# A graph network of four layers on one core: about half of the edges are sorted by source during the hops, and their messages take the source row by a one-hot product instead of a gather

## The chip, the cores and the metric

The kernel runs on one core of a Trainium2 chip. The metric is the time of one execution on the device in microseconds (us); the figure for the kernel before is the median of three executions. A core has five engines that run side by side and wait for each other by semaphores: TensorE (PE, matmuls; the loading of its weights is listed as PEld), VectorE (DVE), ScalarE (ACT), GpSimd (POOL) and SyncE (SP). Every engine takes its instructions in order. Transfers are issued from the queues of SP, ACT and POOL. The chip also grants PE a share of its full clock, which the profile records.

## The reference

Input: x of 3125 nodes by 96 features, 100000 edges (src, dst) sorted by dst, and 4 attributes per edge. Four blocks follow each other, each x = x + block(relu(layernorm(x))):

```
L0: out = h; ten times:  out = 0.9 * segment_sum(out[dst] * w, src) + 0.1 * h        ("hops")
L1: m = relu(h[src]) + eps;  a = softmax of m over the edges of each dst;  (h + segment_sum(a * m, dst)) @ W + b
L2: node    = batchnorm(relu(h @ W_node + b))
    edge    = batchnorm(relu(edge_attr @ W_edge + b))
    message = batchnorm(relu([h[src], h[dst], edge] @ W_msg + b))
    segment_sum(message, dst) + node
L3: two graph convolutions with a leaky relu between
```

L2 is where the change lies. The product with W_msg splits in three: P = h @ W_msg[:96] for the source, Q = h @ W_msg[96:192] + bias for the destination, and the edge's features times W3 (the last 96 rows with the batchnorm folded in). So each edge needs P[src] + Q[dst] + relu(edge_attr @ W_edge + b) @ W3. The sums over all edges that the batchnorm of the messages needs come from a Gram matrix.

## The kernel before

All of it is one function, `narrow`; a second one, `wide`, follows only where a flag says that the data break an assumption of the first (here it does not run). `narrow` has these stages:

- **Setup** (0 to some 440 us): edges are laid out as 98 rows ("quads") of 1024 edges. One-hots of source and destination are multiplied to count matrices (C8, and its transpose A8, in fp8). Tables for later are written to DRAM, among them ea_d (18 rows per edge: attributes as an fp16 high and low half and a one), rl_d and rlT_d (the destination's row within a quad) and srcT_d (the source).
- **Hops** (to 1088 us): L0 as ten products of A8 with the node features. `gather` (L379 to L391) runs 13 slots of two blocks of 128 nodes per step, each block 25 matmuls (L387). `onward` scales the result, and `beside` (L512) puts other work in the slots: the statistics of the edge features (L515 to L522), loading x, and a ReLU over A8 that checks for an overflow (L531). The lists of this and of the next stage are ordered by a scheduler. POOL has no work in this stage.
- **L1** (1088 to 1249 us): one loop over 25 blocks (L619). Each block also computes its rows of P and Q and writes them to the DRAM tables Pt and Qt (L661), as fp16 in two halves: high in columns 0 to 95, low in 96 to 191.
- **Messages** (1249 to 2477 us, L674 to L839), in an order written out by hand (L811 to L837). The 100000 edges are taken in 196 half quads of 512, four chunks of 128 edges each. For half quad i the calls are: `gather_rows(i)` issues four indirect transfers on POOL (L747), each fetching 128 rows of 384 bytes of Pt, five half quads ahead and into six buffers (pgs); `edge_features(i)` makes the features of 512 edges on PE, and ACT and DVE split them into an fp16 high and low half (eh L766, el L768); `messages(i)` runs six matmuls per chunk into PSUM (L781): three for the features times W3 (eh with W3's high and low half, el with the high half), one for Q by a one-hot of the destination (ohT) and two with an identity, which add the gathered halves of P. DVE takes the relu (m, L783), ACT and DVE split m again (L376, L377). `summed(i)` runs two half quads later: per chunk one matmul sums the messages by destination (segs, L801) and one adds to the Gram matrix (gram, L803). `load_quad(g)`, on SP's queue, loads what a quad needs: four pieces of Q (L734), the edge rows (L739) and the destination rows spread over 128 partitions (L741). After each quad the sums are written to the table Sd (L808); rows shared with the next quad are carried over by a small matmul (L800).
- **L3** (2477 us to the end): Sd is loaded, the batchnorm is applied, and two convolutions with C8 follow.

## Time and profile before

| | us |
|---|---|
| median of three runs | 2426.81 (2423.4 to 2430.7) |
| the profiled execution, its own time | 2647.15 |
| its span, first to last instruction | 2645.2 |
| PE busy / DVE / ACT / POOL | 2003.1 / 1433.2 / 870.8 / 808.4 |
| hops, 560 to 1140: PE busy | 573.4 of 580 |
| messages, 1350 to 2480: PE busy, POOL busy | 777.3 and 699.1 of 1130 |
| gathers on POOL (L747) | 784, mean 0.978, first 1248.8, last 2451.7 |

The profiled execution is a run of its own, and longer than the median. A row of the profile names the line, the engine, the operation, out<-in by the program's names, the shapes and the count; after the bar come busy time, mean ns of one, and the engine's idle time just before these instructions with what ended it ("issue": nothing that the profile shows). PE's matmuls overlap, so its busy time adds up overlapping durations only once, and the distance between starts says more than a duration. "Granted clock" is the share of PE's full clock.

### The profile page before, as it was taken

The page shows a single profiled execution, that of the slowest core. Times are in us where ns is not written, and L with a number is a line of the kernel's source. Part 1 is how long each engine was busy: PE and PEld are TensorE (multiplying, and loading weights), DVE is VectorE, ACT ScalarE, POOL GpSimd, SP SyncE. Part 2 cuts the span into 40 slices and gives each one's busy share as a digit, 9 for nine tenths or more (in the row PEclk, how much of TensorE's full clock was granted, in tenths as well). Part 3 has the DMA queues.
Part 4 walks back from the last instruction along what each step waited for, and adds up shares of the span by engine and source line. Part 5 has one row for each costly group of instructions (what it writes and reads, how often), then busy time and mean ns, then how long its engine had stood idle before and what let it go on. Part 6 is the DMA issues. An engine that isn't in the chain of part 4 may idle for free.

```text
span 2645.2 us, 47376 instructions
## 1 busy us (share of the span) xinstructions
PE 2003.1 (76%) x17758; PEld 1553.0 (59%) x17758; DVE 1433.2 (54%) x3971; ACT 870.8 (33%) x2136; POOL 808.4 (31%) x808
## 2 busy tenths in 40 slices
PE   0477777899999999997475666767776776667699
PEld 0222335788888899986354445555555555555488
DVE  2768999875655554876244333434333334334653
ACT  0398846479433311432121111112111111111340
POOL 4100000000000000000666566666666666666000
PEclk9889999999999999998566675556555556555599
DMA  2100000000000000101222222222222222222100
GB/s 74 56 14 1 1 1 1 6 9 10 9 10 10 10 20 2 25 18 26 61 65 68 49 64 68 65 69 64 65 68 65 68 65 68 65 68 65 31 1 21
DMA packets 118578, 100.90 MB, mean 38 GB/s; under 512 B 83532, under 2 KB 90454, under 8 KB 118338
## 3 DMA queue, kind: packets, MB, share of 16 engines
q1 hardware_dynamic: 91002, 54.80, 7.9%
q0 software_dynamic: 25088, 38.59, 6.4%
q10 hardware_dynamic: 2248, 4.40, 0.6%
q8 instruction: 141, 2.31, 0.4%
q14 instruction: 99, 0.81, 0.1%
HBM read 83.46 MB, written 14.21 MB: 37 GB/s over the span
## 4 chain that ended last, share of the span: by engine, by line
PE 39%; issue 18%; DVE 14%; ACT 8%; another core or an unknown queue 5%; SPq 0%; DMA 0%; ACTq 0%; DVEq 0%
PE hop L387 19%; PE pre L781 7%; PE segs L801 3%; DVE u L377 3%; ACT x L531 3%; ACT u L376 2%; PE gram L803 2%; DVE el L768 2%; PE ef L764 2%; DVE m L783 1%; PE eps L520 1%; ACT A L444 1%; PE hop L623 1%; DVE oh L757 1%
## 5 line engine op out<-in xcount | busy, mean ns | idle before, releaser
L747 POOL DMA_INDIRECT u<-Pt,srow x784 | 766.9, 978 | 590.3 <-issue 186.4
L387 PE MATMUL hop<-u,A 128*128 128x192 f16 (+1 forms) x6250 | 550.0, 247 | 3.1 <-DVE degs L481 1.4
L387 PEld LDWEIGHTS <-A 128*128 128x128 fp8e4 x6250 | 522.4, 98 | 48.3 <-issue 44.6
L783 DVE SCALAR_TENSOR_TENSOR m<-pre,cb 128x384 f32<-128x384 f32 x196 | 109.1, 557 | 577.6 <-PE pre L781 287.1
L376 ACT ACTIVATE u<-m 128x384 f16<-128x384 f32 x196 | 102.5, 523 | 881.9 <-issue 721.9
L801 PE MATMUL segs<-u,oh 128*128 128x194 f16 x784 | 239.6, 337 | 126.3 <-issue 76.1
L781 PE MATMUL pre<-u,ident 128*128 128x96 f16 x1568 | 275.8, 267 | 68.9 <-issue 68.0
L781 PE MATMUL pre<-W3h,eh 96*128 96x96 f16 x1568 | 279.8, 269 | 58.4 <-issue 56.9
L272 PE MATMUL cps<-hk,hl 128*128 128x500 f16 x784 | 232.5, 417 | 53.4 <-DVE hl L230 36.7
L803 PE MATMUL gram<-u 128*97 128x194 f16 x784 | 245.4, 344 | 5.4 <-issue 5.4
L230 DVE TENSOR_TENSOR hk<-ki,keyT 128x4000 f16<-128x4000 f16 x98 | 220.3, 2248 | 43.7 <-PE cps L272 27.2
L781 PE MATMUL pre<-qg,ohT 128*128 128x96 f16 x784 | 210.2, 268 | 33.0 <-issue 32.9
L781 PE MATMUL pre<-W3h,el 96*128 96x96 f16 x784 | 210.1, 268 | 30.4 <-issue 27.2
L781 PEld LDWEIGHTS <-eh 96*128 96x128 f16 x1568 | 178.4, 136 | 77.1 <-issue 74.5
L803 PEld LDWEIGHTS <-u 128*97 128x97 f16 x784 | 143.2, 183 | 123.2 <-issue 118.9
L589 POOL IOTA li<- 128x512 f16 x1 | 1.2, 1185 | 680.2 <-ACT exs L507 680.2
L781 PEld LDWEIGHTS <-ident 128*128 128x128 f16 x1568 | 164.9, 135 | 74.0 <-issue 73.9
L276 ACT ACTIVATE C<-cps 128x500 f32 x269 | 162.8, 605 | 91.6 <-PE cps L275 65.8
L801 PEld LDWEIGHTS <-oh 128*128 128x128 f16 x784 | 103.2, 132 | 126.6 <-issue 126.6
L377 DVE TENSOR_TENSOR u<-m,u 128x384 f16<-128x384 f32 x196 | 109.5, 559 | 115.6 <-ACT u L376 59.0
L272 PEld LDWEIGHTS <-hl 128*128 128x128 f16 x784 | 73.8, 119 | 166.1 <-DVE hl L230 77.5
L521 ACT ACTIVATE eps<-eps 96x512 f32<-96x512 f32 x196 | 106.2, 569 | 153.8 <-PE eps L520 145.3
(309 smaller groups left out, 3095.1 us busy)
## 6 DMA issues: line engine op xcount, KB each, us to landing
h<-rl_d SPq DMA_DIRECT2D x98, 256.0 KB
u<-Pt,srow POOLq DMA_INDIRECT x784
qg<-Qt SPq DMA_DIRECT2D x392, 12.0 KB
Sd<-sacc SPq DMA_DIRECT2D x98, 48.0 KB
x<-ea_d SPq DMA_DIRECT2D x195, 18.0 KB
et<-ea_d SPq DMA_DIRECT2D x97, 36.0 KB
et<-in_edge_attr_T ACTq DMA_DIRECT2D x4, 390.6 KB
ea_d<-eh SPq DMA_DIRECT2D x8, 195.3 KB
```

The costliest lines, as they stand in the source:

```text
L230: V.tensor_tensor(t, pat[:, None, :, :].to_broadcast([P, s, n, c]), val[:, q, :].rearrange("p (s c) -> p s c", s=s)[:, :, None, :].to_broa ...
L272: T.matmul(ps, hl[:, j // 4, :, j % 4], hk[:, j // 2, :, j % 2], start=j == js[0], stop=n == 0 and j == js[-1])
L276: S.activation(C8[:, :, bass.ds(column_of(g), WIN)], ps, AF.Copy)
L376: S.activation(hi, t, AF.Copy)
L377: V.tensor_sub(lo, t, hi)
L387: T.matmul(ps[:, i, :], table[:, k, c0 + (b0 + i) * P:c0 + (b0 + i + 1) * P], u[:, k, :], start=k == 0, stop=k == NB - 1)
L521: S.activation(ps, ps, AF.Relu)
L747: G.indirect_dma_start(out=pgs[i % len(pgs)][:, c, :], out_offset=None, in_=Pt, in_offset=bass.IndirectOffsetOnAxis(ap=srow[:, k:k + 1], a ...
L781: T.matmul(ps[:, c, :], t, w, start=j == 0, stop=j == 5)
L783: V.scalar_tensor_tensor(m, ps, 0.0, over_b(cb, HC), ALU.max, ALU.subtract)
L801: T.matmul(seg, oh[:, half, :, c], mm[:, c, :], start=half == 0 and c == 0, stop=last)
L803: T.matmul(gram, mm[:, c, :D + 1], mm[:, c, :], start=i == 0 and c == 0, stop=g == Q - 1 and last)
```

## The change

The first QA = 47 quads (48128 edges) are treated in a new way; the other 51 quads keep their gathers. The 47 quads form three groups GA of 125, 125 and 126 columns of 128 edges.

- **Sorting, during the hops.** `in_bins(g)` is a generator; from slot 13 on `beside` advances it by two steps per slot. Per group it loads src and dst, finds for each edge its bin (25 bins of 125 source rows) and its place in the bin by prefix sums along the rows (13 scans per group, two bins packed in a number) and over the partitions (a matmul with a triangle, tri16), and then POOL issues one indirect scatter per column: 128 records of 12 fp16 numbers (attributes, one, source row in the bin, destination row) to the DRAM table recs[g], 376 scatters in all. The records are blank elsewhere, so bins have spare places: a group fills 152 chunks instead of 125 or 126. Other residents of the scratch room in x shrink (the edge statistics are aggregated in four parts), and x is loaded in slot 106 instead of 91, on SP's queue instead of ACT's.
- **Turning, during L1.** `in_fields(g)` loads recs[g], transposes the records on PE in groups of four units and writes them to the table fields, up to three steps per block from blocks 2, 7 and 16 on. P is also loaded to SBUF in tiles of 125 rows (psb).
- **Messages.** There are now 216 units of four chunks in an alternating list: 114 of sorted edges ("A") and 102 of gathered half quads ("B"). In an A unit a chunk holds edges of a single bin, so P comes from two matmuls of a one-hot of the source (ohS) with psb. Its destinations fall in a window of 128 or 256 rows per slice of 25 chunks (18 slices; WIDE, 13 of one and 5 of two windows), so Q takes two matmuls per window and the sums one per window. Slices hand rows over to the next slice by a shifted product. For both kinds the edge features stay fp32 and take one fp32 matmul with W3 instead of three fp16 ones; eh and el are gone.
- **Around it.** Sums go to two tables Sd, added on POOL before L3. The flag is computed at the end of L1 instead of its start, and counts the edges placed. The mean of the messages is corrected for the EMPTY blank places.

```diff
+QA = 47
+GA = [(0, 125), (16000, 125), (32000, 126)]
+BINS, BN = 25, 125
+SL, CAP = 6, 768
+CG = 152
+UA = len(GA) * CG // 4
+WIDE = [1] * 13 + [2] * 5
...
+    def in_bins(g, rp, ep):
...
+        for i in range(13):
+            V.scalar_tensor_tensor(mv, t, float(i), w, ALU.is_equal, ALU.mult, accum_out=tot[:, i:i + 1])
+            if i % 4 == 3:
+                yield
...
+        T.matmul(ps, tri16, tots.rearrange("p a b -> p (a b)"), start=True, stop=True)
...
+        for i in range(13):
+            V.scalar_tensor_tensor(mv, t, float(i), w, ALU.is_equal, ALU.mult)
+            V.tensor_tensor_scan(scan, mv, mv, tot[:, i:i + 1], ALU.add, ALU.max)
+            V.copy_predicated(pos, mv.bitcast(I32), scan)
+            yield
...
+        for c0 in range(0, C, 14):
...
+            G.dma_start(et, ea[:, c0:c0 + n])
+            G.tensor_copy(r[:, :n, 0:4], et)
+            G.tensor_tensor(r[:, :n, 4:8], et, r[:, :n, 0:4], ALU.subtract)
+            G.tensor_copy(r[:, :n, 9:11], lane2[:, c0:c0 + n, :])
+            for c in range(n):
+                ins = G.indirect_dma_start(
+                    out=recs[g], out_offset=bass.IndirectOffsetOnAxis(ap=addr[:, c0 + c:c0 + c + 1], axis=0),
+                    in_=r[:, c, :], in_offset=None, bounds_check=P * CG - 1, oob_is_err=False)
...
-                        load_x()
...
+                    if slot == 106:
+                        load_x(nc.sync)
+                    for b in range(2 * (slot - 112), min(2 * (slot - 111), NB)) if 112 <= slot < 125 else ():
+                        V.scalar_tensor_tensor(x[:, b, :], hs[:, b, :], back[:, b:b + 1], x[:, b, :], ALU.mult, ALU.add)
+                    if slot >= 13:
+                        next(binning, None)
+                        next(binning, None)
...
-                    if 0 <= i < 50:
-                        S.activation(junk, A8[:, i // 2, i % 2 * (NP // 2):(i % 2 + 1) * (NP // 2)], AF.Relu, bias=late_top,
+                    for i in (2 * i, 2 * i + 1) if 0 <= i < 50 else ():
+                        S.activation(junk, A8[:, i // 4, i % 4 * (NP // 4):(i % 4 + 1) * (NP // 4)], AF.Relu, bias=late_top,
...
+        def in_fields(g):
+            r = lp.tile([P, CG, 12], F16, name="recs2", bufs=2)
+            nc.sync.dma_start(r.rearrange("p c k -> p (c k)"), recs[g].rearrange("(p c) k -> p (c k)", p=P))
...
+                for i in range(n):
+                    T.matmul(ps[:, i, :], rf[:, u0 + i].rearrange("p f j -> p (f j)"), ident16,
+                             start=True, stop=True)
+                t = wp.tile([44, 4, P], F16, name="fts")[:, :n, :]
+                S.activation(t, ps, AF.Copy)
...
+            for j, (first, per) in enumerate(((2, 3), (7, 3), (16, 3))):
+                for _ in range(per if b >= first else 0):
+                    next(turning[j], None)
...
+        UB = (Q - QA) * 2
+        units = sorted([((i + 0.4) / UA, 0, i) for i in range(UA)] + [((i + 0.6) / UB, 1, i) for i in range(UB)])
...
+            for r in (0, 9):
+                nc.sync.dma_start(et[r:r + 9, :], fields[i, :36].rearrange("(f j) e -> f (j e)", f=9))
+            sp = wp.tile([P, 2, HC * P], F16, name="spread", bufs=5)
...
-            eh = wp.tile([D, HC * P], F16, name="eh")
-            S.activation(eh, ps, AF.Relu)
-            el = wp.tile([D, HC * P], F16, name="el")
-            V.scalar_tensor_tensor(el, ps, 0.0, eh, ALU.max, ALU.subtract)
+            feat[n] = wp.tile([D, HC * P], F32, name="efs")
+            S.activation(feat[n], ps, AF.Relu)
...
+                by = [(feat[n][:, cs], W3)]
+                if kind:
+                    pg = pgs[i % len(pgs)]
+                    by += [(hot[n][0][:, cs], quad[QA + i // 2][1][:, i % 2, :]), (ident16, pg[:, c, :D]), (ident16, pg[:, c, D:])]
+                else:
+                    k, s, _, _ = chunk(i, c)
+                    by += [(hot[n][2][:BN, cs], psb[:, k, hl * D:(hl + 1) * D]) for hl in range(2)]
+                    by += [(hot[n][0][:, v, cs], slices[s][1][:, v, hl * D:(hl + 1) * D]) for v in range(WIDE[s]) for hl in range(2)]
...
+            for n in range(L + 2):
+                if n + 1 < L:
+                    edge_features(n + 1)
+                    one_hots(n + 1)
+                if n >= 2:
+                    summed(n - 2)
+                if n < L:
+                    messages(n)
+                if n % 6 == 5:
+                    node_piece(n // 6)
+                if n + 5 < L:
+                    fetch(n + 5)
+                if n < L and units[n][0] and units[n][1] + 5 < UB:
+                    gather_rows(units[n][1] + 5)
...
+            for t, d in ((sd, Sd[0]), (sd2, Sd[1])):
+                nc.sync.dma_start(t[:, b:b + 5, :], d[b * P:(b + 5) * P].rearrange("(b p) d -> p b d", p=P))
+            G.tensor_tensor(sd[:, b:b + 5, :], sd[:, b:b + 5, :], sd2[:, b:b + 5, :], ALU.add)
```

## The prediction

> **What bounds the kernel now.** I read the page first (spans and the forty slices), then the stages by window, then the gather's row, then POOL and PE in order of time inside the message stage.
>
> ```profile
> span 2645.2 us, 47376 instructions
> POOL 4100000000000000000666566666666666666000
> PEclk9889999999999999998566675556555556555599
> L747 POOL DMA_INDIRECT u<-Pt,srow x784 | 766.9, 978 | 590.3 <-issue 186.4
> L387 PE MATMUL hop<-u,A 128*128 128x192 f16 (+1 forms) x6250 | 550.0, 247 | 3.1 <-DVE degs L481 1.4
> ...
> 330.00:480.00 150.00, 113.64 (x942) 69.63 (x941) 141.99 (x322) 89.42 (x243) 0.12 (x1) 0.97 0.00 1
> 560.00:1140.00 580.00, 573.40 (x6275) 519.78 (x6273) 354.06 (x1254) 249.00 (x577) 1.19 (x1) 1.00 0.05 12
> 1140.00:1250.00 110.00, 92.84 (x967) 81.50 (x964) 76.78 (x404) 33.08 (x102) 1.15 (x1) 0.94 0.07 18
> 1350.00:2480.00 1130.00, 777.26 (x6303) 579.15 (x6303) 440.12 (x884) 209.12 (x467) 699.12 (x715) 0.59 0.26 64
> ...
> L747 POOL DMA_INDIRECT u<-Pt,srow x784: 938/944/1372, 1248.8 to 2451.7; - x196
>   DMA Qt<-hv: 153.4, 1
> ...
> 1264.44 0.94 POOL L747 DMA_INDIRECT u<-Pt,srow  x1 [0.30 <-issue]
> 1265.69 0.94 POOL L747 DMA_INDIRECT u<-Pt,srow  x1 [0.30 <-issue]
> ```
>
> The slices show two halves. Up to 1250 us PE works at full clock and POOL does nothing; afterwards POOL issues 784 gathers and PE runs at a granted clock of 0.59. The windows give, in their columns, the length and the busy time of PE, PEld, DVE, ACT and POOL, then the granted clock. In the hops (560 to 1140) PE is the limit, 573 of 580 us. In the message stage no engine is full by this account, so the cadence has to be read: a gather holds POOL 0.944 us and the next starts 0.30 us later, 1.245 us apart whenever nothing is waited for. 784 of them need 976 us; they took 1204 (1248.8 to 2451.7, and the last one).
>
> The difference is of a peculiar kind:
>
> ```profile
> 1263.58 0.24 PE L781 MATMUL pre<-qg,ohT 128*128 128x96 f16 x1 [1.17 <-issue]
> 1265.00 0.24 PE L781 MATMUL pre<-u,ident 128*128 128x96 f16 x1 [1.19 <-issue]
> 1267.10 0.24 PE L781 MATMUL pre<-u,ident 128*128 128x96 f16 x1 [1.85 <-issue]
> ...
> 2520.73 0.80 PE L883 MATMUL op<-W_g,zT 96*128 96x96 f32 x4
> 2521.36 0.25 PE L387 MATMUL hop<-u,C 128*128 128x192 f16 x1
> ```
>
> Here PE, waiting for nothing that is named, steps through single matmuls 1.4 to 2 us apart, and POOL then waits for PE to hand back a gather buffer. POOL's idle time is 590.3 us; without the 153.4 before its first gather and 784 x 0.30 between them, 202 us of such waiting remain. The profiled execution took 2647.15 us, 220 above the median of 2426.81. I take the two for the same thing, an effect of tracing in the stage with the most transfers: 2647 - 202 = 2445, and with 0.944 for the mean of 0.978 per gather 2418; the median lies between them. So without tracing the message stage is taken to last about 1000 us (976 of gathers and 23 from the last gather to the last gram matmul), bound by POOL's cadence. Measured time is predicted as the median of 2427 less what changes.
>
> **The change part by part.**
>
> Removed: the gathers of 47 quads. 784 become 51 x 8 = 408, 408 x 1.245 = 508 us over 216 units (114 of sorted edges, 102 gathered half quads). POOL stops being the limit; PE is next. Two fp16 weight halves and the DVE step L768 (678 ns) go, and one fp32 matmul per chunk takes the place of three fp16 ones.
>
> PE per unit, at full clock. The hops give 550.0 us for 6250 matmuls of 192 columns, 88 ns, so 44 for 96 columns and about 250 for 512. For the fp32 matmul the rows above have the same shape: four records, two products, from 2520.73 to 2521.36, 0.31 us each.
> - Gathered: 0.25 + 4 x (0.31 + 3 x 0.044) + 8 x 0.088 + 0.15 for the carry = 2.87 us.
> - Sorted, window of one: 0.25 + 4 x (0.31 + 4 x 0.044) + 0.70 = 2.89.
> - Sorted, window of two (the last five slices, 32 units): 0.25 + 4 x (0.31 + 6 x 0.044) + 12 x 0.088 = 3.61.
> - 102 x 2.87 + 82 x 2.89 + 32 x 3.61 = 646; 17 slice hand-overs of some 0.9 and the node pieces bring 671. PE was busy 84% of the L1 window, 99% of the hops; I take 92%: 730, and 15 to start and drain: **745 us in place of 1000, -255**.
>
> [...] The trace shows two loads per product and 0.31 us; I take that[...].
>
> Other engines beside PE: DVE, from m 557, lo 559 (L377), oh 683/2 plus overhead 0.42, ohT about 0.33 per 512 columns: 1.99, 2.2 and 2.8 us for the three kinds, 473 us, with the 0.59 us wait for ACT between m and lo 600. ACT 1.1 a unit, 240. SP issues some 2 us of transfers per sorted unit and 4.9 per quad (3.19 for the four qg, 0.33, 1.04, 0.35): 478 us. All lie below 671, five units ahead or two behind. DVE is the nearest.
>
> Hops: 376 scatters of 128 rows, and 27 small loads with three POOL steps. POOL was idle there. Nearest row: the gather, 1.245; with 1.85 for each load and its steps (POOL's cast and subtract of 1000 elements took 1.2 and 2.1 us, these have 56) 468 + 50 = 518 us, 575 if each load's landing (2.1 us) is waited for. In program order they begin near 605 (slot 24, 4.56 us a slot) and end at 1125 to 1180. Two things wait for them: the load of x, SP, at slot 106 (979 us; group 1 must be read, 605 + 250 x 1.245 + 35 = 951) and the third in_fields, b = 16 (1182 us; SP's load and then ACT's copy wait, and PE behind them). Both fit, the second by 2 to 57 us. The bounds for a scatter: none below the gather's 1.245[...]. In the trace, [...]the mean gather is 34 ns over its median, 13 us in all. I take the trace's value and nothing exposed; the range has 0 to 100.
> DVE adds some 265 steps of 126 elements, 0.22 us each (neighbouring fp32 steps 0.15 to 0.31): 58 us, in stretches where it idles 40%. If that cover fails, hop matmuls wait for its PSUM reads. Four offset matmuls wait for DVE with PE's hops queued behind them, 1 to 3 us each: **+8**. Halving the ReLU scan (L531) adds 50 fixed costs to ACT, which is full only from 555 to 675: in the 8. The later x load and x update have 27 us between them, for 1.2 MB (5 us at q1's 262 GB/s): nothing, or 5.
> L1: 29 groups of four transposes on PE (6 us) and an ACT copy each, with one PSUM buffer, so 0.8 us may be exposed each time; PE also loses a hop buffer: 5 to 30, **+15**. The flag and its DVE passes (3 us) now precede the messages: **+4**. The second Sd load and POOL's five adds stand before x += sd: **+5**. Bigger zero fills and blank records before the hops, some 4 MB, lie in a stage in which SP's queue waits 274 us for ACT: nothing; at the rate of queue q1 (54.8 MB in 7.9% of the span, 262 GB/s) they would cost 15 us uncovered.
>
> Sum: 2427 - 255 + 32 = **2204 us**. In the profiled run's own terms 2647 - 202 - 255 + 32 = 2222 plus whatever tracing then adds.
>
> **The rivals.**
> 1. POOL late in the hops: scatters at 1.6 us instead of 1.245 end near 605 + 602 + 50 = 1257, 75 us after the third in_fields asks; x late by about 60. For: the slack is thin. Against: the gather has as many rows. 2204 + 60 to 140: 2260 to 2345.
> 2. A unit's chain through PE, ACT and DVE runs in lockstep[...]: 216 units at 4.0 to 4.5 us, 865 to 970. For: two-deep buffers. Against: m steps in the trace can follow 3.3 us apart (1807.70 and 1810.99). 2330 to 2430.
> 3. Slower: PE keeps the low clock. At half clock the units cost 4.8, 4.85 and 6.1, in sum 1083, and with hand-overs and starts about 1120: 2427 + 120 + 32 = 2580. It decides below a granted clock of about 0.6, where PE's 700 us become the old 1000. For: this very stage was granted 0.59. Against: it was starved then; from 330 to 480, PE busy 114 of 150, the clock was 0.97.
> 4. It does not do what it says: an overfull bin sets the flag and the wide kernel runs as well, a whole second computation, far slower; nothing in the profile speaks to it.
>
> **Numbers.** Main case 0.70 (2090 to 2280: 0.22 us per fp32 product, the least seen, would give 78 less, an 85% busy PE 60 more), rival 1 0.12, rival 2 0.09, rival 3 0.06, rival 4 0.02, no change 0.01. The range 2070 to 2350 holds the main case, rival 1 and the cheap end of rival 2. A measurement here tells about 0.3%. Faster 0.90, same 0.02, slower 0.08.
>
> **What would show it.** 408 gathers, and POOL idle between bursts in the message stage; PE's granted clock there above 0.85; fp32 pre matmuls near 0.31 us a product; scatter rows near 0.94 us, the last before 1180; PE hop at over 95% in the hops; the stage from first to last gram near 750 us, tracing apart. A PE clock near 0.6 there, scatters of 1.3 us and more, or long waits of ACT for recs2 would prove it wrong.

## The result, and the profile after

The changed kernel takes 2438.27 us (median of nine executions, 2388.52 to 2490.94); the kernel before took 2427.70 beside it (2423.40 to 2431.04). One kernel's times spread here with the length of time for which PE's clock stays at half (mean granted clock 0.871 in the execution of 2388.52 us, 0.829 in that of 2490.94), and the comparison counts only executions near the fastest: by those the ratio is 0.9889, 95% interval 0.9854 to 0.9923, a gain of 1.1%. Over all its executions there is no gain. The forecast was 2204.

The profiled execution is the fastest of the nine, 2388.52 us, span 2386.2. First its page: the span, two engine rows of the forty slices, the granted clock, and the groups of the gathers and of the fp32 product.

```profile
span 2386.2 us, 49427 instructions
PE   0467777789999999997996999889999999999498
POOL 5010000000777777774003554243333454441100
PEclk9979999999999999999997596586655798899699
L1001 POOL DMA_INDIRECT h<-Pt,srow x408 | 397.3, 974 | 654.8 <-PE pre L1046 402.0
L1046 PE MATMUL pre<-W,efs 96*128 96x96 f32 x1728 | 448.3, 354 | 0.0
```

POOL is no longer the limit: it issues 408 gathers and waits 402 us for PE's products to free a buffer. PE took its place as forecast, with eights and nines through the message stage (slices 22 to 36). But the clock row has fives and sixes in that stage. The same by windows; the columns are those of the windows shown before (length, busy time of PE, PEld, DVE, ACT, POOL, granted clock, DMA share, GB/s).

```profile
1293.00:1360.00 67.00, 64.05 (x375) 53.05 (x376) 25.99 (x63) 15.15 (x30) 40.92 (x43) 0.50 0.37 93
1360.00:1400.00 40.00, 38.97 (x412) 33.04 (x411) 25.63 (x65) 14.80 (x32) 21.29 (x22) 0.98 0.40 103
...
1650.00:1800.00 150.00, 139.89 (x932) 118.46 (x932) 59.06 (x149) 31.77 (x68) 51.72 (x54) 0.57 0.28 68
...
2100.00:2200.00 100.00, 95.55 (x1067) 84.31 (x1066) 61.11 (x156) 29.90 (x67) 34.81 (x35) 0.95 0.36 84
1293.00:2213.00 920.00, 863.24 (x7297) 740.48 (x7297) 452.52 (x1152) 236.45 (x513) 392.35 (x403) 0.74 0.33 82
```

PE is busy 93% to 97% of each of these windows, but from 1650 to 1800 it gets through 932 matmuls in 150 us, and from 1360 to 1400 through 412 in 40: 6.2 and 10.3 per us. Busy time does not tell these apart, the count and the clock do. In the order of time of PE (start, duration, instruction), one chunk of a sorted unit at half clock and one at full clock:

```profile
1802.65 0.71 PE L1046 MATMUL pre<-W,efs 96*128 96x96 f32 x2
1803.15 0.37 PE L1046 MATMUL pre<-u,ohS 125*128 125x96 f16 x2
...
1803.48 0.71 PE L1046 MATMUL pre<-W,efs 96*128 96x96 f32 x2
...
1961.34 0.42 PE L1046 MATMUL pre<-W,efs 96*128 96x96 f32 x2
1961.60 0.25 PE L1046 MATMUL pre<-u,ohS 125*128 125x96 f16 x2
...
1961.78 0.42 PE L1046 MATMUL pre<-W,efs 96*128 96x96 f32 x2
```

From start to start the fp32 product takes 0.50 us at half clock and 0.26 at full, and a chunk 0.83 against 0.44.

The waits of the stage (what waits, for what, us in total, times, longest) show the pauses of PE:

```profile
PE segA L1092 <- DVE sh L1089: 35.9, 16, 4.8
PE ef L932 <- DVE hT L929: 15.7, 7, 2.3
```

The first is a slice hand-over: the shift matrix sh is made on DVE only when `summed` reaches the hand-over, behind the one-hots and the messages' steps. The second is a node piece, whose scaling (L929) stands in DVE's list directly ahead of its transposes. Each of the 13 falls of the clock inside the stage comes within 2.2 us of the end of such a pause, of 1.56 us or more each, or inside it. The pauses add up to 51.6 us; that they cost far more than their own length is what the runs below show. The stage also begins at half clock: the clock fell at 1276.7 us, between short waits at the end of L1, and PE then waits 7.8 us for the first spread of fields.

By stages, from the same executions:

| | before, us | after, us | difference | forecast |
|---|---|---|---|---|
| end of the hops | 1087.4 | 1098.4 | +11 | +8 |
| L1, first to last of its products | 145.4 | 172.0 | +27 | +15 |
| to the first feature matmul | 19.8 | 20.6 | +1 | +4 |
| message stage | 1001 | 919.7 | -81 | -255 |
| from there to the end | 170.6 | 173.6 | +3 | +5 |

The 1001 is worked out: the median 2427 less the other rows of the profile before (1253.8 to the first feature matmul and 170.6) and the 2 us between span and time. The profile before has 1220.8 there; why, is told below.

### The profile page after: what moved, and what is told of

It reads as the page before. It is cut to its first block, busy times and chain, and to the rows that moved or that the text cites. A ratio compares the mean times of both kernels' runs of the same rounds, so it can differ in the third digit from the quotient of the medians.

```text
span 2386.2 us, 49427 instructions
## 1 busy us (share of the span) xinstructions
PE 2053.4 (86%) x18466; PEld 1685.0 (71%) x18466; DVE 1499.8 (63%) x4538; ACT 924.9 (39%) x2283; POOL 853.9 (36%) x928
## 4 chain that ended last, share of the span: by engine, by line
PE 43%; DVE 6%; ACT 2%; issue 1%; DMA 0%; SPq 0%; POOL 0%; DVEq 0%; ACTq 0%
PE pre L1046 20%; PE hop L409 4%; PE gram L1064 4%; PE ef L1028 4%; PE segA L1094 3%; PE segs L1073 3%; PE hop L805 2%; ACT u L398 1%; DVE u L399 1%; DVE m L1048 1%; PE segs L1072 1%; PE op L1177 1%; PE segA L1092 0%; ACT hb L394 0%; PE pq L837 0%
## 5 line engine op out<-in xcount | busy, mean ns | idle before, releaser
L1001 POOL DMA_INDIRECT h<-Pt,srow x408 | 397.3, 974 | 654.8 <-PE pre L1046 402.0
L1046 PE MATMUL pre<-W,efs 96*128 96x96 f32 x1728 | 448.3, 354 | 0.0
L1046 PEld LDWEIGHTS pre<-W,efs 96*128 96x128 f32 x1728 | 345.0, 248 | 4.3 <-issue 4.3
L552 POOL DMA_INDIRECT recs<-rec,x x250 | 247.1, 988 | 179.4 <-DVE wt L634 103.5
L1046 PE MATMUL pre<-qa,ohTA 128*128 128x96 f16 x1166 | 147.4, 233 | 0.0
L663 DVE BATCH_NORM_STATS2 x<-eps 96x6 f32<-96x512 f32 x196 | 134.4, 686 | 18.7 <-ACT eps L662 16.3
L632 DVE SCALAR_TENSOR_TENSOR wt<-hop,sc,h 128x96 f32<-128x96 f32 x225 | 69.7, 310 | 116.9 <-PE hop L409 116.9
L552 POOL DMA_INDIRECT recs<-rec,addr x126 | 123.9, 983 | 38.6 <-issue 36.3
L1046 PE MATMUL pre<-u,ohS 125*128 125x96 f16 x912 | 137.5, 240 | 0.0
L1030 ACT ACTIVATE efs<-ef 96x512 f32<-96x512 f32 x216 | 124.6, 577 | 29.7 <-PE ef L1028 29.7
```

Source lines behind the costliest of these rows:

```text
L552: ins = G.indirect_dma_start(out=recs[g], out_offset=bass.IndirectOffsetOnAxis(ap=addr[:, c0 + c:c0 + c + 1], axis=0), in_=r[:, c, :], in_ ...
L663: V.bn_stats(stats[:, i % 49, :], ps)
L1001: G.indirect_dma_start(out=pgs[i % len(pgs)][:, c, :], out_offset=None, in_=Pt, in_offset=bass.IndirectOffsetOnAxis(ap=srow[:, k:k + 1], a ...
L1046: T.matmul(ps[:, c, :], t, w, start=j == 0, stop=j == len(by) - 1)
```

## The experiments

Theory 1: PE's clock goes to half after a short pause, and comes back only when PE streams enough columns in a short interval; the fp32 products with their weight loads (two per product, 248 ns each in the mean of the profile after, against 114 to 159 for those of the fp16 products) leave a unit just short of that, so PE stays at half clock although it never rests. The rivals: the clock is set by the stage's transfers and POOL (Theory 2), or fp32 products are simply dear (Theory 3), or PE draws too much (Theory 4).

**Three fp16 products again** (trio), all else as changed:

```diff
-            feat[n] = wp.tile([D, HC * P], F32, name="efs")
-            S.activation(feat[n], ps, AF.Relu)
+            eh = wp.tile([D, HC * P], F16, name="eh")
+            S.activation(eh, ps, AF.Relu)
+            el = wp.tile([D, HC * P], F16, name="el")
...
+            V.scalar_tensor_tensor(el, ps, 0.0, eh, ALU.max, ALU.subtract)
...
-                by = [(feat[n][:, cs], W3)]
+                eh, el, _ = feat[n]
+                by = [(eh[:, cs], W3h[:, :D]), (eh[:, cs], W3h[:, D:]), (el[:, cs], W3h[:, :D])]
```

> The changed kernel with one part undone: edge features times W3 as three fp16 products again (with the DVE step for the low half, placed after the one-hots), everything else kept. Theory 1 (PE's clock is granted by how many columns it streams in a short window; the fp32 products with their slow weight loads leave a unit at half clock at about 0.80 of the possible columns, too few to get back to full clock): a unit at half clock falls from about 4.9 to 3.9 us and its streamed share rises above 0.9, so PE returns to full clock after each stall: granted clock of the message stage above 0.9 (0.73 in the changed kernel), units then set by DVE at 3.2 to 3.6 us, stage 700 to 790 us instead of 919, time 2220 to 2320. Theory 2 (the clock is low because of the stage's transfers or POOL, not because of PE's pattern): clock stays near 0.7, stage about 830 to 900 us. Theory 3 (fp32 products are dear at any clock, and nothing else is wrong): full-clock units hardly change (2.9 to 2.7 us) and the clock stays below 0.8.

2263.01 us (2260.83 to 2270.89), ratio 0.9342 (0.9319 to 0.9366). The message stage by windows:

```profile
1295.00:2085.00 790.00, 629.13 (x8161) 517.29 (x8161) 568.30 (x1367) 234.78 (x513) 396.34 (x403) 0.89 0.37 95
```

The clock is 0.89 (expected: above 0.9) and the stage 789.8 us. PE's clock falls 23 times inside the stage, oftener than before the edit (13), and is back within 3 to 14 us each time but the last, which runs on into the next stage. Units at full clock, in the median: about 3.1 us (sorted, one window), 3.98 (two windows) and 2.56 (gathered), against 2.86, 3.53 and 3.00 with fp32. So at full clock fp32 costs a gathered unit 0.44 us, and the sorted units are even faster with it (with the trio PE waits 41.3 us for DVE's el). Its main cost is that with it PE does not get back to full clock as soon: stretches at half clock of up to 153.6 us in the profile after, of 3 to 14 us here but for the last. Theory 3 falls.

**The pauses taken away** (nostall): the shift matrices are made one unit ahead, a node piece is scaled two units ahead. No work is added or removed.

```diff
             for n in range(L + 2):
+                if 1 <= n <= L:
+                    shift_ahead(n - 1)
...
+                if n % 6 == 3 and 0 < n // 6 - len(COLS) <= len(COLS):
+                    c0, w = COLS[n // 6 - len(COLS) - 1]
+                    rT = hTs[:D, 2 * c0:2 * c0 + 2 * w].bitcast(F32)
+                    V.tensor_scalar(rT, rT, held[0][0], held[0][1], ALU.mult, ALU.add)
```

> The changed kernel with the two stalls of PE ahead of which the clock falls taken away: the shift matrices of the slice hand-overs are made on DVE one unit earlier, and DVE scales a node piece two units before its transposes. No work is added or removed. Theory 1: PE falls to half clock only after a pause, so fewer than half of the 14 falls of the message stage remain; the clock there rises from 0.73 to 0.85 or more, the stage from 919 to 780 to 850 us, and the spread between runs (2388 to 2491) shrinks; the first 70 us stay at half clock, since nothing changes there. Theory 2: the clock stays at 0.7 to 0.75; only the stalls themselves (some 50 us, of which part is taken up elsewhere) go, so 870 to 910 us.

2227.33 us in the median, single executions 2153.23, 2221.16, 2233.49 and 2267.12. Four falls inside the stage are left, all after a wait for the copy-out of a slice of two windows. The spread did not shrink, and its cause is in the profiled execution (the slowest of the four):

```profile
1299.00:1530.00 231.00, 230.81 (x1540) 193.21 (x1540) 96.94 (x242) 56.50 (x119) 103.12 (x108) 0.57 0.30 78
1530.00:1850.00 320.00, 318.08 (x3511) 276.18 (x3511) 221.69 (x574) 115.31 (x254) 202.29 (x209) 1.00 0.46 120
```

PE does not pause in the first window, and for 1.0 us in all in the second. Begun at half clock, it stays there until 1495.9 us; once up, it holds full clock to the end of the second window. The unit list is the same all the while, and the faster window has the higher DMA share.

**Useless work added** (filler4):

```diff
             ps = p2.tile([P, 512], F32, name="ef")[:D, :]
+            for _ in range(4):
+                T.matmul(ps, ident16[:, :D], li[:, 0].rearrange("p m c -> p (m c)"), start=True, stop=True)
             T.matmul(ps, We, got[n][0], start=True, stop=True)
```

> The changed kernel with useless work added: ahead of each unit's feature matmul PE runs four more 128-row, 512-column fp16 matmuls into the same PSUM tile (overwritten by the real one). At full clock they cost 4 x 0.22 = 0.85 us a unit, 184 us in the stage; at half clock twice that. Theory 1: a half-clock unit now streams about 0.86 of the possible columns, so PE gets back to full clock soon after each stall: clock 0.9 or more, units 3.7 to 4.4 us, stage 820 to 900 us, that is no slower than the 919 without the extra work, perhaps faster. Theory 2 (transfers) and Theory 3: clock unchanged near 0.73, the stage longer by 184/0.73 = 250 us, near 1170. Theory 4 (the clock is cut because PE draws too much): clock below 0.73, stage above 1170.

2392.84 us (2380.21 to 2395.68), ratio 0.985 (0.9817 to 0.9883), stage 923.6 us:

```profile
1293.00:2215.00 922.00, 880.48 (x8154) 673.42 (x8154) 455.26 (x1150) 262.38 (x512) 389.43 (x403) 0.95 0.32 82
```

The stage is a little longer than the 820 to 900 that Theory 1 gave, and far from the 1170 of the others. With 864 long matmuls more, it lasts as long as without: the clock went from 0.74 to 0.95 and pays for them. Theory 4 falls, since more work would have lowered the clock.

**Gathers left out** (nogather):

```diff
-                G.indirect_dma_start(out=pgs[i % len(pgs)][:, c, :], out_offset=None, in_=Pt,
-                                     in_offset=bass.IndirectOffsetOnAxis(ap=srow[:, k:k + 1], axis=0))
+                pass
```

> The changed kernel without the 408 gathers of the message stage: the gathered units read what lies in the buffers, so their messages are other values; every other instruction stays. POOL and its queue are then idle in this stage. Theory 1: PE's pattern is unchanged, so clock 0.70 to 0.76 and stage 900 to 920 us. Theory 2 (POOL and the gathers' transfers hold the clock down): clock above 0.9 and stage 700 to 780 us.

2371.39 us (2365.91 to 2440.23), ratio 0.9782 (0.9746 to 0.9818). The profiled execution is the slowest of five:

```profile
1294.00:2264.00 970.00, 914.07 (x7297) 781.70 (x7295) 450.75 (x1150) 237.27 (x512) 0.00 (x0) 0.69 0.20 57
```

With POOL at rest and the traffic cut from 82 to 57 GB/s the clock of this execution is no better. The 970 us lie outside the 900 to 920 expected, on the side that Theory 2 excludes. The other four executions were 58 to 74 us shorter, which puts their stage at an estimated 896 to 912 us, far from the 700 to 780 of Theory 2. The traffic that is left does not hold the clock down either: nostall had full clock at a DMA share of 0.46. Theory 2 falls.

**Every cause of half clock seen so far taken away** (steady): the version without pauses, with useless matmuls while PE idles ahead of the stage, and with two banks for slices of two windows, so that PE does not wait for their copy-out.

```diff
+            keep_busy(36)
             edge_features(0)
+            keep_busy(12)
...
-                seg = segA if WIDE[s] == 2 else segA[s % 2:s % 2 + 1]
+                seg = [segA[s % 2][:, v, :] for v in range(WIDE[s])]
+                if first and WIDE[s] == 2:
+                    T.matmul(segA[s % 2], ident16, none16, start=True, stop=False)
```

> The version without the two stalls, and two causes of half clock more taken away: 36 useless matmuls of 512 columns before the stage's first feature matmul, where PE idles for 7.6 us, and 12 after it, so that the stage starts at full clock; and the slices with two windows alternate between two PSUM banks (both windows in one bank, opened by a product with zeros), so that PE does not wait for their copy-out, before which the four remaining falls lay. Theory 1: all units at full clock, 82 x 2.86 + 102 x 3.00 + 32 x 3.53 = 653 us and some 15 for hand-overs and node pieces: stage 660 to 690 us at a clock above 0.97, time 2135 to 2170 in every run, spread below 20 us. If the clock were set by chance or by heat and not by pauses, the clock would stay near the 0.82 of the version without stalls and the spread near its 114 us (2153 to 2267).

With it ran the same version with one pause put back (onelate), the same with the fp16 trio for gathered units alone (steady_mixed), and one part of the change alone, the fp32 product in the kernel before (before_fp32):

> The steady version with one pause put back: the shift matrix of one hand-over (slice 2, about unit 36 of 216) is made late again, so that PE stalls once for 2 to 4 us near 1400 us. If a pause costs only its own length: 3 us more than the steady version, within 0.3% of it. Theory 1: the clock falls there and stays at half until a window happens to be full enough; in the version without stalls such a stretch lasted 55 us on the mean and up to more than 100, each losing 0.4 of its length: 10 to 100 us more than the steady version, differing from run to run, with one long stretch of 0.5 from about 1400 us.

> The steady version with the fp16 trio for the gathered units only (DVE is lighter loaded there), fp32 for the sorted ones. Full-clock units as measured: sorted 2.86 and 3.53 us with fp32, gathered 2.56 with the trio: 82 x 2.86 + 32 x 3.53 + 102 x 2.56 = 608, with hand-overs 620 to 650 us for the stage and 2090 to 2130 for the kernel, if DVE (about 2.45 us a unit with the low half) does not become the limit; if it does, no gain over the steady version or a few new pauses.

```diff
-                for j, (t, w) in enumerate(((eh[:, cs], W3h[:, :D]), (eh[:, cs], W3h[:, D:]), (el[:, cs], W3h[:, :D]),
-                                            (o, qg[:, i % PER, :]), (ident16, pg[:, c, :D]), (ident16, pg[:, c, D:]))):
+                for j, (t, w) in enumerate(((half_[i][:, cs], W3), (o, qg[:, i % PER, :]), (ident16, pg[:, c, :D]), (ident16, pg[:, c, D:]))):
```

> The kernel before with one part of the change alone: one fp32 product with W3 instead of three fp16 ones, without the DVE step for the low half. If the kernel before is bound by POOL's gather cadence of 1.245 us in its message stage, as the prediction read it: no change, within 1% (2405 to 2440), as PE needs 4.8 us a half quad at half clock and POOL 4.98. If PE at half clock is the limit there: 1.1 us more a half quad, 196 of them, 2550 to 2640. The profile of this run also tells whether the message stage lasts 1000 us or the 1220 of the first profile.

All four ran on another chip, and there the kernel before took 2651.13 us (2646.66 to 2654.64), not 2425. steady took 2812.27 (ratio 1.0569, 1.0513 to 1.0625), onelate 2790.64 (1.0533, 1.0494 to 1.0572), steady_mixed 2772.98 (1.0466, 1.0443 to 1.0489): all slower than before. The time went in the hops, which ended at 1581.4 us in steady instead of 1098. By windows of steady on that chip:

```profile
640.00:700.00 60.00, 8.65 (x28) 2.75 (x27) 4.89 (x25) 5.73 (x12) 43.84 (x54) 0.50 0.04 4
780.00:840.00 60.00, 59.04 (x616) 50.39 (x614) 43.28 (x131) 59.23 (x134) 0.00 (x0) 1.00 0.05 10
880.00:940.00 60.00, 7.51 (x22) 2.30 (x22) 1.18 (x8) 0.00 (x0) 46.48 (x56) 0.50 0.03 4
```

and of trio on the first chip, the same stretch of the same code:

```profile
640.00:700.00 60.00, 56.85 (x562) 47.70 (x560) 47.95 (x156) 56.81 (x127) 47.04 (x55) 0.94 0.08 15
```

While POOL issues scatters back to back, PE starts 28 matmuls in 60 us on the one chip and 562 on the other; where POOL rests, the one chip too does 616. The scatters themselves go at the same pace on both (1.284 and 1.283 us apart in the median). PE's steps there:

```profile
725.96 0.32 PE L409 MATMUL hop<-u,A 128*128 128x192 f16 x1 [1.09 <-issue]
728.08 0.32 PE L409 MATMUL hop<-u,A 128*128 128x192 f16 x1 [1.80 <-issue]
```

These are steps like those of the profile before, waits of 1 to 2 us that nothing named ends. before_fp32 took 2649.43 us (ratio 0.9993, 0.9978 to 1.0008): on this chip the message stage of the kernel before is not set by PE's products.

**The same again**, on a third chip, where the kernel before took 2650.98 us (2643.28 to 2656.78), with the kernel before as a kernel of its own:

> The steady version once more (both stalls gone, the stage started at full clock, two banks for two-window slices). In the last comparison all engines crept whenever POOL issued indirect transfers back to back, in the kernel before too (2651 us instead of 2425), which hid the effect. Where the kernel before takes about 2425 us, Theory 1 expects as before: stage 660 to 690 us at a clock above 0.97, 2135 to 2170 us, spread below 20 us. Where it takes about 2650, the hops will again last about 1140 us instead of 656, and the kernel 2780 to 2830.

> The steady version with the fp16 trio for gathered units only, once more. Where the kernel before takes about 2425 us: 2090 to 2130 us if DVE does not become the limit; else as the steady version. Where it takes about 2650: about 2770 again.

> The steady version with one late hand-over, once more. Where the kernel before takes about 2425 us: by the length of the pause alone 3 us over the steady version; by Theory 1 10 to 100 us over it, with one stretch at half clock from about 1400 us. Where it takes 2650: within the noise of the steady version, as in the last comparison (2783 to 2808 beside 2783 to 2831).

> The kernel before, unchanged, for another profile. The prediction took the 220 us between the profile (2647) and the median (2427) for tracing. If that is right, a profile is again near 2647 with the median near 2427 on the same chip. If it is the chip, the profile's time agrees with the other runs of the same chip; where that is 2425, the message stage lasts about 1000 us with gathers 1.245 us apart, and PE shows no waits of 1.4 to 2 us that end by nothing named.

steady2 2794.08 (ratio 1.053, 1.049 to 1.057), mixed2 2761.34 (1.0424, 1.0396 to 1.0451), onelate2 2783.09 (1.0483, 1.0446 to 1.052; one execution took 2926.38). before_again took 2650.57, and its page has the picture of the profile before:

```profile
span 2648.7 us, 47376 instructions
POOL 4100000000000000001665566666666666666000
PEclk9889999999999999998566556565566565655699
```

Here the profiled execution (2650.48) is no longer than the others (2643 to 2657). So the 2647 of the first profile needs no effect of tracing: its picture is that of this chip, on which all 13 executions of the kernel before took 2643 to 2657 us. Which chip it came from is not on record.

**steady and the changed kernel side by side**, on a chip with the kernel before at 2425.39 us (2419.86 to 2430.79):

> The steady version a third time, now beside the changed kernel itself. Where the kernel before takes about 2425 us: Theory 1, stage 660 to 690 us at a clock above 0.97, 2135 to 2170 us with a spread below 20; a clock left to chance would give 2150 to 2270 and the spread of the version without stalls. Where the kernel before takes 2650: 2776 to 2831 again.

> The changed kernel, unchanged, beside the steady version. Where the kernel before takes about 2425 us: 2388 to 2491 again. Where it takes 2650, the hops creep beside the 376 back-to-back scatters in this kernel as in the steady one, 480 us longer than the 656 of the first profile, and the message stage is as slow or slower: 2388 + 480 = about 2870, between 2830 and 3000, so slower than before by 7 to 13%.

after_again: 2324.24, 2432.77, 2446.16 and 2462.22 us, one of them below the range expected. steady3: 2130.52 us (2128.53 to 2140.41), ratio 0.8801 (0.8781 to 0.8821). Its message stage by windows:

```profile
1299.00:1400.00 101.00, 101.00 (x1080) 85.33 (x1079) 67.12 (x166) 38.50 (x82) 76.07 (x77) 1.00 0.51 125
1400.00:1600.00 200.00, 199.00 (x2196) 172.65 (x2193) 140.74 (x369) 72.38 (x160) 126.53 (x131) 1.00 0.50 120
1600.00:1800.00 200.00, 200.00 (x2240) 174.32 (x2240) 134.83 (x343) 71.32 (x158) 124.62 (x129) 1.00 0.49 118
```

Full clock throughout, 656.6 us from the first feature matmul to the last gram, the units at 2.86, 3.53 or 3.00 us by their kind in the median. The other stages are those of the changed kernel. The time lies 5 us below the range expected, since hand-overs and node pieces cost less than the 15 us put down for them. The profiled execution of after_again spent 984.4 us on the stage, at a clock of 0.68, with stretches of half clock of up to 160 us. Theory 1 stands: with all products of the messages kept, and some useless ones added, the stage is 263 us shorter than in the first profile after. The spread is 12 us, against 138 for the changed kernel beside it.

**One pause put back, the trio for gathered units, and L1 without the turning**, on a chip with the kernel before at 2425.81 us:

```diff
-                if last and s:
+                if last and s and s != 2:
                     for d in range(WIDE[s - 1]):
                         shifts[s, d] = wp.tile([P, P], F32, name="sh", bufs=2)
...
+                        if s == 2:
+                            shifts[s, d] = wp.tile([P, P], F32, name="sh", bufs=2)
+                            V.tensor_scalar(shifts[s, d], lane, gaps[:, d, s - 1:s], part, ALU.add, ALU.is_equal)
```

> The steady version with one late hand-over (slice 2). Where the kernel before takes about 2425 us: if a pause costs only its length, 2131 to 2136. By Theory 1 the clock falls once near 1410 us and stays at half for a stretch that differs from run to run: 2140 to 2230, spread above 20 us, one long stretch at 0.5 in the stage. Where the kernel before takes 2650: as the steady version there.

2152.51 us in the median, single executions 2136.17, 2137.02, 2149.96, 2155.05, 2155.05 and 2192.54; ratio 0.8859 (0.8832 to 0.8886). The profiled execution is one of the two cheap ones. PE in order of time:

```profile
1404.87 0.24 PE L1081 MATMUL gram<-u 128*97 128x194 f16 x1
1407.02 0.74 PE L1113 MATMUL segA<-saccA,sh 128*128 128x96 f32 x2 [1.90 <-DVE sh L1109]
1407.55 0.37 PE L1115 MATMUL segA<-u,ohA 128*128 128x194 f16 x1
1407.71 0.37 PE L1081 MATMUL gram<-u 128*97 128x194 f16 x1
```

A wait of 1.90 us, and the same instruction takes 0.24 ahead of it and 0.37 behind it: the clock is at half at once. Here it came back after 14 us. Two shorter waits did the same: later in this profile 0.71 us for a one-hot and 0.28 for messages, within 3 us, were followed by 3.4 us at half clock, and in noturn below 0.72 and 0.28 by 14 us. By the median the one pause cost 22 us over steady3 (from another chip with the same time before), by the dearest execution 62, for 1.9 us of waiting; the executions spread over 56 us, those of the two versions on the same chip without the late hand-over (below) over 13. The "long" stretch that was expected shows only in the times of the others, not in this profile.

> The steady version (2130 us, stage 660 at full clock) with the fp16 trio for gathered units only. Where the kernel before takes about 2425 us: a gathered unit at full clock falls from 3.00 to 2.56 us, 102 x 0.44 = 45 us less: 2085 to 2105 us, if DVE is not the limit. If DVE's low half makes PE wait, pauses come back and the clock falls below 0.95 in the stage: 2120 to 2160. Where the kernel before takes 2650: 2748 to 2785 again.

```diff
+            if units[n][0]:
+                t = feat[n].bitcast(F16)
+                feat[n] = (t[:, :HC * P], t[:, HC * P:], ps)
+                S.activation(feat[n][0], ps, AF.Relu)
+            else:
+                S.activation(feat[n], ps, AF.Relu)
```

2121.80 us (2111.45 to 2124.16), ratio 0.8739 (0.8719 to 0.876), the best of the versions that do the whole work. The stage is 643.5 us at 0.98, between the two cases expected: 45 us were to be had, 13 came, as DVE's low half made PE wait again (3.06 us at 1439, and three waits of about a microsecond), with three short falls of the clock. It beats the kernel before (2425.81 here) and the changed one (2324 to 2491 in all its executions, where the kernel before took 2420 to 2431). On the two chips where that took 2650 it was 4.2% and 4.7% slower.

> The steady version without the turning in L1: the 114 transposes of records on PE and their 29 copies on ACT are left out and zeros are written to the table instead, so the sorted messages have other values. Loads, the field copies, the writes and all other instructions stay. L1 lasts 30 us longer in the changed kernel than in the one before (172 to 141). If transposes and copies, which share ACT and one PSUM buffer with the block's own chain, make that up: L1 near 145 to 155 us and 20 to 27 us less in all. If it is the rest (loads of the sorted records, the field copies on ACT of 2.8 us each, the loads of P to SBUF, a late POOL): at most 8 us less.

```diff
-                    T.matmul(ps[:, i, :], rf[:, u0 + i].rearrange("p f j -> p (f j)"), ident16,
-                             start=True, stop=True)
-                t = wp.tile([44, 4, P], F16, name="fts")[:, :n, :]
-                S.activation(t, ps, AF.Copy)
+                t = zeros[:, :n, :]
```

2121.55 us (2115.73 to 2128.47), ratio 0.8738 (0.8718 to 0.8757), 9 us less than steady3 (on another chip), just over the 8 that the second case allowed. In the profiles L1's products last 159.4 us, against 175.8 in steady3, from which noturn was made, 172.0 in the changed kernel and 145.4 in the one before: transposes and copies are some 13 to 16 us of the added 27 to 30. What the other 14 are was not separated; the windows of noturn still show DVE at 121 us against 113 and ACT at 59 against 51 before.

## Why the prediction was wrong

**The clock.** The step that failed is "PE per unit, at full clock", and with it the term "745 us in place of 1000". The units at full clock were costed well: 2.87, 2.89 and 3.61 forecast, 3.00, 2.86 and 3.53 measured, and 4.8, 4.85 and 6.1 at half clock against 4.91, 5.23 and 5.87. But 52% of the 919.7 us were spent at half clock. That is rival 3, and at only part of its strength. It was given 0.06 for a bad reason: "it was starved then" explained the low clock of the stage by a lack of work, and the window put against it (330 to 480) could not tell. By the count explained next it streams only 0.61 of the possible columns on the mean. Its clock fell twice, came back at once after an interval full of matmuls of 500 columns (0.99 and 1.04), and then met no interval under 0.45. PE busy was taken for the thing that raises the clock.

Being occupied is not enough: PE was occupied 139.89 of 150 us in the profile after (1650 to 1800) and 230.81 of 231 us in nostall, both at a clock of 0.57. The trace shows what goes with a rise. The clock is full or half, in stretches that are multiples of 3.41 us (in the profile after, stretches at half of 3.41, 10.24, 44.37 and 153.60 us). For each interval of 3.41 us of the message stage I counted the columns that its matmuls stream, as a share of 2.4 columns per ns at full clock and 1.2 at half: in filler4 the useless matmuls of 512 columns follow each other 0.216 us apart at full clock and 0.427 at half. An fp32 product counts as four times its columns. That is an estimate from the profile after: at half clock an fp16 product of 96 columns (h by the identity, L1046) takes 80 ns from start to start instead of 41, 39 more; an fp32 product of 96 columns whose weights are a single column (the carry, L1072) takes 411 ns from its start to that of the next matmul instead of 258, 153 more, which is 3.9 times the 39. The table gives the range of 5% to 95% of the intervals and in brackets the median; "half, then full" are those after which the clock rose.

```
                 half, then full    full, then half    stays half, median    stays full
after            .81-.90 (.86)      .00-.43 (.26)      .80                   .53-.82 (.74)
nogather         .85-.91 (.87)      .10-.47 (.31)      .80                   .56-.79 (.74)
nostall          .80-.90 (.86)      .08-.38 (.30)      .80                   .69-.86 (.74)
filler4          .80-.91 (.89)      .12-.42 (.33)      .75                   .62-.85 (.81)
trio             .87-.98 (.93)      .00-.36 (.14)      .39                   .53-.89 (.70)
before_again     .82-.99 (.92)      .02-.44 (.26)      .57                   .48-.68 (.52)
```

By these counts there are two levels. Most rises come after an interval of about 0.85 or more (medians 0.86 to 0.93) and most falls after one of about 0.43 or less (medians 0.14 to 0.33); between them the clock mostly stays what it is. At full clock the units of the changed kernel stream 0.74 in the median, and the clock stays. At half clock an fp32 product takes 0.50 us, of which four times 96 columns would fill an estimated 0.32, and the 0.80 of such units is mostly not enough. In onelate3 the interval with the late hand-over holds 0.32 and the clock falls; the next four hold 0.79, 0.84, 0.75 and 0.86, and after the last of these it is full again. Hence one unit list has two speeds, 2.9 and 5.0 us a unit, each lasting until an interval happens to be fuller or a pause comes. The levels are an estimate from these counts, and where an interval begins within the trace is known to the width of a matmul or two. The lower one separates well: of 766 intervals of these six profiles at full clock that kept it, 3 hold 0.43 or less. The upper one does not: of 661 at half clock that kept it, 79 hold 0.85 or more. So columns are a measure that fits, not one that is shown to be what the chip counts.

**The tracing.** The 202 us of PE's steps in the profile before were taken for an effect of tracing. The conclusion drawn from it, 1000 us for the stage by POOL's cadence on the chip of the median, fits the sum of the stages (1001); the reason was wrong. Such steps showed in the profiles from the two chips on which the kernel before took 2643 to 2657 us in every execution. The document has times from such chips and from others, and the prediction mixed them: it took durations from the one and the total from the other. That did not make the miss: up to the message stage POOL issues no indirect transfer in the kernel before, and the profile shows none of these steps there (no wait of PE of 1 us or more that nothing named ends before 1248 us; 131 in the message stage, 192 us). That its other stages last as long on the chip of the median was assumed and not seen, as no profile of the kernel before came from such a chip.

**POOL's gathers and scatters.** Right: 408 gathers, POOL idle between bursts. A scatter costs nearly what a gather does, and none was held up for long (the mean of all 376, 987 ns, is 9 over the median, 3 us in all; the gather's mean here is 974); the rows, minimum, median and maximum in ns, first and last start:

```profile
L552 POOL DMA_INDIRECT recs<-rec,x x250: 967/978/1279, 589.2 to 932.3; - x125
L552 POOL DMA_INDIRECT recs<-rec,addr x126: 970/977/1108, 938.1 to 1106.9; - x126
```

From start to start they are 1.283 us apart in the median, against the gather's 1.245. The last starts at 1106.9, before the forecast's 1125 to 1180, and nothing waits longer than 3.3 us for it. Rival 1 is false where the kernel before takes 2425 us. Where it takes 2650 its place was right, the hops, but not its mechanism: POOL kept its pace, 1.284 us in steady, while PE, DVE and ACT were busy 8.65, 4.89 and 5.73 of 60 us (640 to 700). The changed kernel itself did not run there; three versions of it lost 4.2% to 5.7%.

**fp32 products.** Taken at 0.31 us, measured 0.26 at full clock and 0.50 at half. Rival 2's ranges (865 to 970 us for the stage, 2330 to 2430 in all) hold the profiled 919.7 and 2388.52, but by luck: with the two-deep buffers kept, steady3 runs its units at 2.86 to 3.53 us, so there is no lockstep of 4 us.

**The small terms.** Hops +8 was +11, the seam +4 was +1, the tail +5 was +3. L1's +15 was mis-sized: +27, near the top of its bound of 30. With PE at full clock all the while, "92% busy" was too careful: the stage takes 657 us, not 745.

## What to carry to other kernels

A busy PE does not tell its speed (93% of 150 us at 6.2 matmuls per us, 97% of 40 at 10.3): read the granted clock beside the count of matmuls in each window, and where a stage was at half clock, cost its units at both clocks. If a unit streams too little to climb at half clock but enough to hold full clock (here 0.80 and 0.74 by the count above), the chance of a pause decides the time; then the cheapest work is to remove the pauses (here 1.56 to 4.76 us at the falls of the profile after; make small operands a unit ahead, give an accumulator a second bank) and to enter the stage at full clock, even with useless matmuls in an idle gap (steady3 has both: 656.6 us for the stage, 919.7 without). And compare a profile's time with other executions on the same chip before calling the difference an effect of tracing.

## What was not expected of the hardware

- The clock's two levels, estimated above: from one unit list, 231 us at 0.57 and 320 us at 1.00 in nostall, with 1.0 us of pauses in both together; in onelate3 a single wait of 1.90 us was followed by half clock, and useless matmuls paid for themselves (864 of them, 923.6 against 919.7 us).
- Chips differed. On two of the four that the experiments ran on, PE, ACT and DVE nearly stop while POOL issues indirect transfers back to back (21 to 59 matmuls in windows of 60 us, against 562 and 632 in trio on another). The DMA engines were not full then: their share was 0.03 to 0.04, and a packet of a scatter took 15 ns in the median, as it did in the profile after. The kernel before took 2643 to 2657 us on those two and 2420 to 2431 on the others. In steady's message stage, where the gathers come in bursts with pauses, PE had only 10 such waits of a microsecond or more, 11 us together, but the clock fell 11 times and the stage took 879.0 us at 0.81. What makes it was not found.
